# Reordering layers 0 to 2 of a four-layer graph kernel: projections, row factors, exponentials, means, tests and the next layer's features

## The chip, the cores and the metric

The kernel runs on one core of a Trainium2 chip. The metric is the device time of one execution in microseconds (us). A profile of one execution names the engines PE (TensorE, its matmuls), PEld (TensorE's loads of the stationary operand), DVE (VectorE), ACT (ScalarE), POOL (GpSimd) and SP (SyncE, which only issues transfers). L861 means line 861 of the kernel before; the program's line numbers shift a little after the change.

## The reference

The input is x, 32 batches of 512 nodes with 64 features, and one normalised adjacency matrix of 512 x 512 with few non-zero entries. Each of the four layers is `x = x + layer(relu(layernorm(x)))`:

```python
# layer 0: graph convolution
out = h @ weight_self + (adj @ h) @ weight_neighbor + bias
# layer 1: two steps of it, with a relu after each
z = relu((adj @ z) @ weights[i])            # i = 0, 1
# layer 2: graph attention
Wh = h @ W.T;  e1 = Wh @ a[:64];  e2 = Wh @ a[64:]
e   = leaky_relu(e1[:, :, None] + e2[:, None, :], 0.2)
att = softmax(where(adj > 0, e, -9e15), axis=-1)
out = elu(att @ Wh)
# layer 3 (flow): 8 heads of attention with s = (hW)(hW).T * graph, where zero
# entries are masked, then a ninth attention over the joined heads
```

All arithmetic is in float32.

## The kernel before

**Stages.** The program has two forms; the one that runs here (`fast_form`) first does layers 0, 1 and 2, some 488 us, and then layer 3, called flow, up to the end. The diff touches the first stage only, and those steps of flow that are done within it. Batches go in 16 pairs (M = 16); 512 nodes are 4 blocks (C) of 128 partitions, so that the x of a pair is 128 x 512.

**Slots.** `slot(k)` for k = 0 to 16 is one step of a pipeline written out by hand: it does layer 0 of pair k, layer 1 of pair k-2, the norm of layer 2 of pair k-3, the preparation of layer 2's attention of pair k-4 (`Gat.prepare`) and its scores and values for pair k-5 (`scores`, `values`). What PE, DVE and ACT do is in the order in which it is written (a manual schedule on these three engines); POOL only adds the bias of layer 0 (L1126). A slot may end with one more piece of work (`more`): in slots 6, 8, 10 and 12 this is `judge_rows(c)`, which tests one block of rows of the adjacency against the form that `fast_form` supposes, and in slot 15 `judge`, which brings the tests to one number.

**Drain.** After slot 16 `drain()` brings the last four pairs through layer 2; its attentions are called g2 (pair 12), g1, g0 and last (pair 15). It has fills (`fill(n)`, matmuls whose result is not used), and ahead of `last.scores(1)` it runs nine periods of flow, -10 to -2, in a loop.

**Steps and names.**
- `centre` (L857): sum of each row over its 64 features (`mean`, L861), times 1/F (L862), x minus mean (L863). It is used by the norms (`Norm.a`) and at the end of an attention (`rest`).
- `Norm.square` squares on ACT (`sq`, L881); `Spread` gathers the squares of up to four norms: `add` sums them (`var`, L899), `root` takes the square root on ACT (`std`, L906), `turn` the reciprocal (`rstd`, L914); `Norm.relu` multiplies (L885).
- `flipped` transposes on PE and copies on ACT (`ht0`, `ht2`, L310 and L312); `neighbours` multiplies by the adjacency (`nt_ps`, L921), `copied` brings this to SBUF on ACT (`nt0`, `nt1`, `nt1b`, L928); `project` multiplies by weights (L941): `po0` for layer 0, `po1a` and `po1b` for the two steps of layer 1. `po0` is added to x in the next slot (L1133), `po1b` in `ends` (L1112).
- `Gat.flip` makes `ht2`. `Gat.prepare`: features `wh_ps` (L967), 16 short matmuls on 64 rows of the array; row factors `e1` (`e_ps`, L974), two matmuls on 64 rows; then on ACT `v`, `q` and `c` (L984 to L990), of which `c` is exp of the row factors. `weigh` (L995) multiplies features by v.
- `Gat.scores` (L1005, DVE), `Gat.values` (`acc` L1018, `den` L1027, PE), `keep` (two copies on ACT, L1037), `back` (transposes to `den_ps` L1048 and `op_ps` L1053), `read` (reciprocal and product `o`, L1063 to L1066), `rest` (`e` = exp(o) on ACT, L1074; then on DVE L1077, L1078, the last of which needs e; then `centre` and a square, L1080).
- PSUM: the pool `ps_t` has four banks, which nt_ps, the transposes, wh_ps and e1 take in turn in the order in which they are written; a bank is free when the copy that reads it is done.
- Flow's `features(step)` of a batch: on ACT `less` (minus the mean, L509), x minus mean with relu (L512), times rstd (L519), times root_d (`hs`, L524); on POOL a difference `hd` (L528); on DVE a maximum `least` (L530). `make_hx` transposes hs (`hx_ps`, L310, copy L312), `make_g` multiplies (`g_ps` L550, copy L562); layer 3 begins with `s_ps` (L383), of which DVE takes maxima (L395).

Of the kernel before, what the change touches and what calls it, by code (L numbers as in the profile page):

```python
# [8 lines left out]
F32 = mybir.dt.float32  # L9
AF = mybir.ActivationFunctionType  # L10
OP = mybir.AluOpType
# [11 lines left out]
def fast_form(  # L23
# [128 lines left out]

    BC = B * C
    least = const.tile([P, BC + 1], F32, name="least")
    sound = const.tile([P, 2 + 2 * C], F32, name="sound")
    unsound = const.tile([1, 1], F32, name="unsound")
    least_out = const.tile([P, B // 2], F32, name="least_out")
    E_MAX = 5.0
# [11 lines left out]
    def scales():  # L170
# [24 lines left out]
            )  # L195
        nc.scalar.copy(urow, ps)

    def judge_rows(c):
        both, t = row_pair("edge"), row_pair("t")[:, 0]
        ok, edge = both[:, 1], both[:, 0]  # L200
        nc.vector.tensor_scalar(edge, adj_f[:, c], 0.0, None, op0=OP.not_equal)
        nc.vector.scalar_tensor_tensor(
            t, urow, root_d[:, c : c + 1], edge, op0=OP.mult, op1=OP.mult
        )
        nc.vector.tensor_tensor(t, t, adj_f[:, c], OP.subtract)
        nc.vector.scalar_tensor_tensor(t, t, -1.0, t, op0=OP.mult, op1=OP.max)
        nc.vector.scalar_tensor_tensor(
            ok, adj_f[:, c], 4e-7, t, op0=OP.mult, op1=OP.is_ge
        )
        nc.vector.scalar_tensor_tensor(  # L210
            edge, adj_t[:, c], 0.0, edge, op0=OP.not_equal, op1=OP.is_equal
        )
        nc.vector.tensor_reduce(
            sound[:, 2 + C + c : 3 + C + c], both.rearrange("p k n -> p (k n)"), AX.X, OP.min
        )


# [7 lines left out]
    def halves(k):  # L225
        return slice(k * F, (k + 1) * F)

    def row_pair(name):

        return pairs_of[0].tile([P, 2, N], F32, name=name, tag="row")  # L230
# [5 lines left out]
        return acc_of[0].tile(shape, F32, name=name, tag=acc_of[1])  # L236

    def judge():
        own = tiny.tile([P, 1], F32, name="own")
        nc.vector.tensor_reduce(own, sound, AX.X, OP.min)  # L240
        ps = acc("own_ps", [1, P])
        nc.tensor.transpose(ps, own, ident)
        nc.vector.tensor_reduce(unsound, ps, AX.X, OP.min)
        nc.vector.tensor_scalar(unsound, unsound, 0.0, None, op0=OP.is_equal)
# [244 lines left out]
    class Heads(Pair):  # L489
# [12 lines left out]
        def features(self, step):  # L502
            b = self.b
            if self.i:
                return
            mean, rstd = (t[:, b % 2] for t in flow_stats[b // 2])
            if step == 0:
                less = tiny.tile([P, C], F32, name="less")
                nc.scalar.mul(less, mean, -1.0)  # L509
                h = Heads.hn[b] = early.tile([P, C, F], F32, name="hn3", bufs=5)  # L510
                for c in range(C):
                    nc.scalar.activation(  # L512
                        h[:, c], xs[b // G][:, b % G, c], AF.Relu, bias=less[:, c : c + 1],
                        scale=1.0,
                    )
            elif step == 1:
                h = Heads.hn[b]
                for c in range(C):
                    nc.scalar.mul(h[:, c], h[:, c], rstd[:, c : c + 1])  # L519
            elif step == 2:  # L520
                h = Heads.hn[b]
                hs = Heads.hs[b] = early.tile([P, C, 2, F], F32, name="hs3", bufs=2)
                for c in range(C):
                    nc.scalar.mul(  # L524
                        hs[:, c], h[:, c, None].to_broadcast([P, 2, F]), root_d[:, c : c + 1]
                    )
# [315 lines left out]
    with (  # L842
# [14 lines left out]
        def centre(to, i):  # L857

            x4 = pair_of(i)
            mean = tiny.tile([P, 2, C], F32, name="mean", bufs=B // 2 + 12)  # L860
            nc.vector.tensor_reduce(mean, x4, AX.X, OP.add)  # L861
            nc.vector.tensor_scalar(mean, mean, 1.0 / F, None, op0=OP.mult)  # L862
            nc.vector.tensor_tensor(  # L863
                to, x4, mean[:, :, :, None].to_broadcast([P, 2, C, F]), OP.subtract
            )
            return mean

        class Norm:
# [81 lines left out]
        class Gat:  # L950
# [8 lines left out]
            def prepare(self):  # L959


                self.wh_ps = [
                    ps_t.tile([P, C, F + 1], F32, name="wh_ps", tag="ps") for k in range(2)
                ]
# [7 lines left out]
                e1 = [ps_t.tile([P, N], F32, name="e1_ps", tag="ps") for k in range(2)]  # L972
                for k in range(2):
                    nc.tensor.matmul(  # L974
                        e1[k], lhsT=wa1[halves(k), :], rhs=self.ht[halves(k), :],
                        start=True, stop=True,
                    )
                self.v = work.tile([P, 2 * C, F + 32], F32, name="v")
                self.q = tiny.tile([P, 2 * C], F32, name="q")
                self.c = row_pair("c")  # L980
                for k in range(2):
                    e2 = self.wh_ps[k][:, :, F]
                    some = slice(k * C, (k + 1) * C)
                    nc.scalar.activation(  # L984
                        self.v[:, some, F:], e2[:, :, None].to_broadcast([P, C, 32]),
                        AF.Exp, scale=0.2,
                    )
                    nc.scalar.activation(self.q[:, some], e2, AF.Exp, scale=0.8)
                for k in range(2):
                    nc.scalar.activation(self.c[:, k], e1[k], AF.Exp, scale=-0.8)  # L990
# [48 lines left out]

            def end(self):  # L1040
                self.read()
                self.rest()

            def back(self):
# [14 lines left out]
            def read(self):  # L1059
# [8 lines left out]
                    rec[:, :, :, None].to_broadcast([P, 2, C, F]), OP.mult,  # L1068
                )

            def rest(self):
                o = self.sq
                e = row_pair("e")[:, 0].rearrange("p (k c f) -> p k c f", k=2, c=C)
                nc.scalar.activation(e, o, AF.Exp)  # L1074
# [3 lines left out]
                nc.vector.scalar_tensor_tensor(x4, e, 1.0, x4, op0=OP.min, op1=OP.add)  # L1078
# [43 lines left out]
        def slot(k, more):  # L1122
# [49 lines left out]
            if n:  # L1172
                n.a()
                n.square()
                some.append(n)
            some += ended
            ended.clear()
            s = Spread()
# [10 lines left out]
            for n in some:  # L1189
                if isinstance(n, Gat):  # L1190
                    flow_stats[n.i] = n.mean, n.rstd
                else:
                    n.relu()
            if l0:
                po0[k] = project([(ht0, ws2), (nt0, wn2)], "po0")
            if u:
                u.back()
                turned.append(u)
# [13 lines left out]
        def drain():  # L1212
# [13 lines left out]
            g2.scores(1)  # L1226
            z = middle(nt1)
            g1.prepare()
            nt1b[M - 1] = neighbours(lambda c: z[:, c, :])
            s = Spread()  # L1230
            s.add(n)
# [3 lines left out]
            nt1b[M - 1] = copied(nt1b[M - 1], "nt1b")  # L1235
            g2.values()
            g2.keep()
            g1.weigh()
            s.turn()
            n.relu()  # L1240
# [7 lines left out]
            g0.flip()  # L1248
            g2.back()
            g2.read()  # L1250
            g1.scores(1)
            g0.prepare()
            fill(3)
            s = Spread()
            s.add(n)
            s.root()
            g1.values()
            g1.keep()
            s.turn()
            n.relu()  # L1260
            last = Gat(M - 1, n2.pop(M - 1).h)
# [3 lines left out]
            g0.scores(0)  # L1265
            g1.back()
            g1.read()
            last.prepare()
            g0.scores(1)
            fill(6)  # L1270
            g0.values()
# [5 lines left out]
            s.add(g2)  # L1277
            g0.back()
            g0.read()
            for i in range(-10, -1):  # L1280
                flow_period(i)
            last.scores(1)
            fill(3)
            last.values()
# [2 lines left out]
            s.add(g1)  # L1287
            last.back()
            last.read()
            last.rest()  # L1290
            fill(6)
            s.add(g0)
# [12 lines left out]
        with tc.manual_schedule(  # L1305
# [12 lines left out]
                4: scales,  # L1318
            }
            for c in range(C):  # L1320
                begun[6 + 2 * c] = lambda c=c: judge_rows(c)
            begun[7 + 2 * C] = judge
            for k in range(M + 1):
                slot(k, begun.get(k))
# [32 lines left out]
def general_form(  # L1357
# [116 lines left out]
    def stats(pool, g):  # L1474
        xg = xs[g]
        nb = G * C
        x3 = xg.rearrange("p b c f -> p (b c) f")
        mean = tiny.tile([P, nb], F32, name="mean", bufs=NG + 1)
# [437 lines left out]
```

## Time and profile before

| | us |
|---|---|
| three runs | 2078.73, 2072.11, 2077.57 |
| their median | 2077.57 |
| the profiled execution, its own time | 2077.25 |
| its span (first to last instruction) | 2075.3 |
| PE busy in the span | 1984.9 (96%) |
| DVE busy | 1748.6 (84%) |
| ACT busy | 1320.3 (64%) |
| POOL busy | 1445.5 (70%) |

The mean clock granted to PE is 0.981 of full speed. In the rows of profile below, a group or a timeline row has its start (in the timeline), busy time, engine, line, operation, output and inputs by the program's names, partitions x elements, and in brackets how long the engine was idle before it and what it waited for. "x16" means 16 instructions joined to one row. A wait row has: who waits, for what, us in total, times, the longest.

### The profile page before, as it was taken

Reading aid. Unit: us, or ns where it says so; the run is one execution under the profiler, and the core shown is the slowest. Engines: PE = TensorE matmul, PEld = TensorE weight load, DVE = VectorE, ACT = ScalarE, POOL = GpSimd, SP = SyncE. Lnnn points to the kernel's source line nnn. Section 1 sums busy time; section 2 is a strip of 40 time slices with the busy share of each in tenths; the row PEclk is TensorE's granted clock in tenths of the full one; section 3 lists DMA queues with packets and bytes.
Section 4 is the critical chain, followed back from the end, with each engine's and each line's share of the span. In section 5 each row is a group of like instructions: output and inputs, shape, how many; then the busy total and the mean of one; then the engine's idle time right before and its main releaser. Section 6 shows DMA issues by size and latency. Waiting matters only on the chain.

```text
span 2075.3 us, 29298 instructions
## 1 busy us (share of the span) xinstructions
PE 1984.9 (96%) x9374; PEld 738.2 (36%) x9374; DVE 1748.6 (84%) x4102; ACT 1320.3 (64%) x2008; POOL 1445.5 (70%) x834
## 2 busy tenths in 40 slices
PE   7999999877999999999999999999999999999995
PEld 4544445432333333333333333333333333333332
DVE  6688887667889898988888988888888988988994
ACT  3444444444676777677777777777777777776674
POOL 2000000002898989898989999998888988888996
PEclk9999999998999999999999999999999999999998
DMA  4000000001222323232223232332223222222233
GB/s 121 1 1 1 1 1 0 1 1 28 71 79 74 83 76 85 68 83 79 78 78 77 75 83 77 79 83 69 79 74 76 72 75 76 75 71 77 77 83 79
DMA packets 185876, 128.05 MB, mean 62 GB/s; under 512 B 124985, under 2 KB 130273, under 8 KB 185585
## 3 DMA queue, kind: packets, MB, share of 16 engines
q1 hardware_dynamic: 166480, 125.30, 22.4%
q10 hardware_dynamic: 18720, 0.59, 0.5%
q8 instruction: 76, 1.25, 0.3%
q14 instruction: 88, 0.71, 0.1%
q0 software_dynamic: 512, 0.20, 0.1%
HBM read 119.48 MB, written 5.37 MB: 60 GB/s over the span
## 4 chain that ended last, share of the span: by engine, by line
PE 60%; POOL 6%; DMA 4%; DVE 3%; issue 1%; ACT 1%; SPq 0%; ACTq 0%; POOLq 0%; DVEq 0%
PE s_ps L383 21%; PE av L438 20%; PE tot_ps L450 6%; PE y_ps L568 5%; POOL p_att L416 5%; PE gT_ps L613 5%; PE g_ps L550 3%; DMA topb<-top_row 2%; DVE p_att L395 2%; POOL p_att L420 1%; DVE p_att L432 1%; DMA top_row<-top 1%; PE hx_ps L310 1%; ACT e_ps L429 1%; DMA recb<-rec_row 0%
## 5 line engine op out<-in xcount | busy, mean ns | idle before, releaser
L416 POOL TENSOR_TENSOR p_att<-p_att,topb 128x1024 f32<-128x1024 f32 x429 | 1007.7, 2381 | 0.0
L395 DVE CUSTOM_DVE_ANT_0 p_att<-s_ps,flow_neg 128x512 f32<-128x512 f32 x1152 | 726.0, 685 | 96.5 <-PE s_ps L383 95.4
L383 PE MATMUL s_ps<-g,hx 64*128 64x512 f32 x2048 | 516.0, 613 | 17.1 <-DVE p_att L432 13.9
L420 POOL TENSOR_TENSOR p_att<-p_att,topb 128x512 f32<-128x512 f32 x286 | 360.5, 1281 | 170.7 <-DMA topb<-top_row 131.8
L429 ACT ACTIVATE p_att<-p_att 128x1024 f32<-128x1024 f32 x288 | 304.8, 1059 | 162.1 <-POOL p_att L420 81.4
L432 DVE TENSOR_TENSOR p_att<-e_ps,p_att 128x1024 f32<-128x1024 f32 x288 | 338.3, 1197 | 32.4 <-ACT e_ps L429 31.4
L429 ACT ACTIVATE e_ps<-p_att 128x1024 f32<-128x1024 f32 x288 | 293.0, 1029 | 79.0 <-POOL p_att L416 68.8
L383 PEld LDWEIGHTS s_ps<-g,hx 64*128 64x128 f32 x2048 | 174.9, 186 | 329.3 <-DVE top L395 175.5
L438 PE MATMUL av<-p_att,hd 128*64 128x512 f32 x1024 | 269.7, 605 | 1.1 <-DVE o_att L487 1.1
L438 PE MATMUL av<-p_att,hn 128*64 128x512 f32 x1024 | 263.3, 592 | 0.0
L1126 POOL TENSOR_TENSOR x<-x,bias_b 128x512 f32<-128x512 f32 x16 | 20.3, 1275 | 307.2 <-DVE hn L863 307.2
L586 DVE SCALAR_TENSOR_TENSOR cat<-y_ps,bh,cat 128x512 f32<-128x512 f32 x256 | 180.0, 745 | 15.5 <-ACT cat L578 14.1
L562 ACT COPY g<-g_ps 128x512 f32<-128x512 f32 x128 | 132.0, 1139 | 85.6 <-PE g_ps L550 85.6
L578 ACT ACTIVATE cat<-y_ps,bh 128x512 f32<-128x512 f32 x256 | 161.2, 681 | 36.3 <-PE y_ps L568 35.9
L450 PE MATMUL tot_ps<-p_att,ones 128*32 128x512 f32 x1152 | 155.6, 605 | 4.3 <-DVE p_att L432 4.3
L568 PE MATMUL y_ps<-o_att,wh_sb 64*128 64x512 f32 x512 | 137.5, 594 | 0.0
L613 PE MATMUL gT_ps<-cat,wo_sb 128*64 128x512 f32 x512 | 131.6, 592 | 0.0
L438 PEld LDWEIGHTS av<-p_att,hn 128*64 128x64 f32 x1024 | 73.9, 137 | 145.8 <-issue 145.8
L438 PEld LDWEIGHTS av<-p_att,hd 128*64 128x64 f32 x1024 | 62.4, 136 | 166.5 <-issue 135.9
L921 PE MATMUL nt_ps<-adj_t,hn 128*128 128x512 f32 x256 | 118.8, 608 | 0.8 <-DVE hn L885 0.8
L487 DVE TENSOR_TENSOR o_att<-av,recb 128x512 f32<-128x512 f32 x144 | 99.0, 688 | 24.4 <-DMA recb<-rec_row 23.7
L528 POOL TENSOR_TENSOR hd<-hn 128x128 f32<-128x128 f32 x32 | 14.7, 460 | 128.5 <-ACT hn L519 128.5
(192 smaller groups left out, 2190.5 us busy)
## 6 DMA issues: line engine op xcount, KB each, us to landing
topb<-top_row SPq DMA_DIRECT2D x288, 256.0 KB
recb<-rec_row SPq DMA_DIRECT2D x288, 128.0 KB
out_dram<-y SPq DMA_DIRECT2D x32, 128.0 KB
x<-in_x_dram SPq DMA_DIRECT2D x3, 1024.0 KB
top_row<-top SPq DMA_DIRECT2D x144, 4.0 KB
parts<-tot SPq DMA_DIRECT2D x144, 4.0 KB
parts<-tot ACTq DMA_DIRECT2D x144, 4.0 KB
rec_row<-rec_flow SPq DMA_DIRECT2D x144, 4.0 KB
```

The lines of the kernel that those rows point to most:

```text
L383: nc.tensor.matmul(ps[:, k], lhsT=x[halves(k), r * P : (r + 1) * P], rhs=g[halves(k), :], start=True, stop=True,)
L395: nc.vector.tensor_tensor_reduce(out=self.p[r][:, k], in0=ps[:, k], in1=flow_neg[:, r], scale=-1.0, scalar=BIG, op0=OP.add, op1=OP.min, ac ...
L416: engine.tensor_tensor(self.p[r], self.p[r], self.topb, OP.subtract)
L420: engine.tensor_tensor(p, p, self.topb[:, k], OP.subtract)
L429: nc.scalar.activation(to, self.p[r], AF.Exp, scale=-1.0)
L432: nc.vector.tensor_tensor(self.p[r], self.joined, self.p[r - 1], OP.add)
L438: nc.tensor.matmul(self.av[halves(k), :], lhsT=self.v(k, j) if j % 2 else self.less_next(k, j), rhs=self.p[j][:, k], start=(j == 0), stop= ...
L450: nc.tensor.matmul(ps[q : q + 32, :], lhsT=ones, rhs=self.p[2 * e + 1][:, k], start=True, stop=True,)
L568: nc.tensor.matmul(ps, lhsT=wh_sb[halves(k), 2 * self.i + k, :], rhs=self.o[halves(k), :], start=True, stop=True,)
L578: nc.scalar.activation(self.cat[:, k], self.y[k], AF.Identity, bias=bh01[:, h : h + 1], scale=0.01)
L586: nc.vector.scalar_tensor_tensor(self.cat[:, k], self.y[k], bh[:, h : h + 1], self.cat[:, k], op0=OP.add, op1=OP.max,)
L613: nc.tensor.matmul(self.gps[halves(k), :], lhsT=wo_sb[:, h, :], rhs=Heads.cat.pop((self.b + k, h)), start=(h == 0), stop=(h == H - 1),)
```

## The change

In a slot, the projection `po0` of layer 0 is issued ahead of `values` instead of after it. In `Gat.prepare`, the two matmuls of the row factors stand ahead of the sixteen of the features. `Gat.exp` is split off from `rest`: in a slot it comes at the same place as before, in the drain it follows `read` at once. `centre` leaves out the multiplication by 1/F, and two operations of 128 x 256 with the factor -1/F take the place of the subtraction of 128 x 512. The test of a block of rows is split into `judge_rows`, at the ends of slots 5, 7, 9 and 11, and `count_rows`, at the ends of 6, 8, 10 and 12; the counts come from accumulator outputs, so that the reduction over 1024 elements (L213) goes, and `judge` compares the counts with 512. In the drain, the nine periods of flow stand at six places instead of one.

```diff
     def judge_rows(c):
-        both, t = row_pair("edge"), row_pair("t")[:, 0]
-        ok, edge = both[:, 1], both[:, 0]
+        both = judged[c] = row_pair("edge")
+        edge, t = both[:, 0], both[:, 1]
         nc.vector.tensor_scalar(edge, adj_f[:, c], 0.0, None, op0=OP.not_equal)
         nc.vector.scalar_tensor_tensor(
             t, urow, root_d[:, c : c + 1], edge, op0=OP.mult, op1=OP.mult
         )
         nc.vector.tensor_tensor(t, t, adj_f[:, c], OP.subtract)
+
+    def count_rows(c):
+        both = judged.pop(c)
+        edge, t = both[:, 0], both[:, 1]
+        at = 2 + C + 2 * c
         nc.vector.scalar_tensor_tensor(t, t, -1.0, t, op0=OP.mult, op1=OP.max)
         nc.vector.scalar_tensor_tensor(
-            ok, adj_f[:, c], 4e-7, t, op0=OP.mult, op1=OP.is_ge
+            t, adj_f[:, c], 4e-7, t, op0=OP.mult, op1=OP.is_ge,
+            accum_out=sound[:, at : at + 1],
         )
         nc.vector.scalar_tensor_tensor(
-            edge, adj_t[:, c], 0.0, edge, op0=OP.not_equal, op1=OP.is_equal
-        )
-        nc.vector.tensor_reduce(
-            sound[:, 2 + C + c : 3 + C + c], both.rearrange("p k n -> p (k n)"), AX.X, OP.min
+            edge, adj_t[:, c], 0.0, edge, op0=OP.not_equal, op1=OP.is_equal,
+            accum_out=sound[:, at + 1 : at + 2],
         )
...
     def judge():
+        counts = sound[:, 2 + C :]
+        nc.vector.tensor_scalar(counts, counts, float(N), None, op0=OP.is_equal)
...
-                nc.scalar.mul(less, mean, -1.0)
+                nc.scalar.mul(less, mean, -1.0 / F)
...
         def centre(to, i):
             nc.vector.tensor_reduce(mean, x4, AX.X, OP.add)
-            nc.vector.tensor_scalar(mean, mean, 1.0 / F, None, op0=OP.mult)
-            nc.vector.tensor_tensor(
-                to, x4, mean[:, :, :, None].to_broadcast([P, 2, C, F]), OP.subtract
-            )
+            for k in range(2):
+                nc.vector.scalar_tensor_tensor(
+                    to[:, k], mean[:, k, :, None].to_broadcast([P, C, F]), -1.0 / F, x4[:, k],
+                    op0=OP.mult, op1=OP.add,
+                )
...
             def prepare(self):
+                e1 = [ps_t.tile([P, N], F32, name="e1_ps", tag="ps") for k in range(2)]
+                for k in range(2):
+                    nc.tensor.matmul(e1[k], lhsT=wa1[halves(k), :], rhs=self.ht[halves(k), :], ...)
                 self.wh_ps = [ ... ]
...
-                e1 = ...        # the same two matmuls, here
...
             def end(self):
                 self.read()
+                self.exp()
                 self.rest()
+            def exp(self):
+                self.e = row_pair("e")[:, 0].rearrange("p (k c f) -> p k c f", k=2, c=C)
+                nc.scalar.activation(self.e, self.sq, AF.Exp)
             def rest(self):
-                e = row_pair("e")[:, 0].rearrange("p (k c f) -> p k c f", k=2, c=C)
-                nc.scalar.activation(e, o, AF.Exp)
+                o, e = self.sq, self.e
...
         def slot(k, more):
+            if l0:
+                po0[k] = project([(ht0, ws2), (nt0, wn2)], "po0")
             some += ended
             s = Spread()
             ...                 # s.add, u.values(), s.root(), keep, weigh, s.turn, relu
-            if l0:
-                po0[k] = project([(ht0, ws2), (nt0, wn2)], "po0")
             if u:
                 u.back()
...
         def drain():
             g1.prepare()
+            flow_period(-10)
+            flow_period(-9)
...
             g2.keep()
+            flow_period(-8)
...
             g2.read()
+            g2.exp()
             g1.scores(1)
             g0.prepare()
+            flow_period(-7)
+            flow_period(-6)
             fill(3)
...
             g1.keep()
+            flow_period(-5)
...
             g1.read()
+            g1.exp()
             last.prepare()
+            flow_period(-4)
+            flow_period(-3)
             g0.scores(1)
             fill(6)
...
             g0.read()
-            for i in range(-10, -1):
-                flow_period(i)
+            g0.exp()
+            flow_period(-2)
             last.scores(1)
...
             last.read()
+            last.exp()
             last.rest()
...
+                begun[5 + 2 * c] = lambda c=c: judge_rows(c)
-                begun[6 + 2 * c] = lambda c=c: judge_rows(c)
+                begun[6 + 2 * c] = lambda c=c: count_rows(c)
```

More of the change, by code (lines that the diff above doesn't have):

```diff
@@ L154, in fast_form @@
     least = const.tile([P, BC + 1], F32, name="least")
-    sound = const.tile([P, 2 + 2 * C], F32, name="sound")
+    sound = const.tile([P, 2 + 3 * C], F32, name="sound")
     unsound = const.tile([1, 1], F32, name="unsound")
@@ L196, in scales @@
         nc.scalar.copy(urow, ps)
+    judged = {}
     def judge_rows(c):
-        both, t = row_pair("edge"), row_pair("t")[:, 0]
-        ok, edge = both[:, 1], both[:, 0]
+        both = judged[c] = row_pair("edge")
+        edge, t = both[:, 0], both[:, 1]
         nc.vector.tensor_scalar(edge, adj_f[:, c], 0.0, None, op0=OP.not_equal)
@@ L859, in centre @@
             x4 = pair_of(i)
-            mean = tiny.tile([P, 2, C], F32, name="mean", bufs=B // 2 + 12)
+            mean = tiny.tile([P, 2, C], F32, name="sum", bufs=B // 2 + 12)
             nc.vector.tensor_reduce(mean, x4, AX.X, OP.add)
-            nc.vector.tensor_scalar(mean, mean, 1.0 / F, None, op0=OP.mult)
-            nc.vector.tensor_tensor(
-                to, x4, mean[:, :, :, None].to_broadcast([P, 2, C, F]), OP.subtract
-            )
+            for k in range(2):
[3 more added lines that the diff above has]
+                )
             return mean
@@ L959, in prepare @@
             def prepare(self):
+                e1 = [ps_t.tile([P, N], F32, name="e1_ps", tag="ps") for k in range(2)]
+                for k in range(2):
+                    nc.tensor.matmul(
+                        e1[k], lhsT=wa1[halves(k), :], rhs=self.ht[halves(k), :],
+                        start=True, stop=True,
+                    )
                 self.wh_ps = [
@@ L971, in prepare @@
                         )
[L972 to L977, printed above, removed]
                 self.v = work.tile([P, 2 * C, F + 32], F32, name="v")
@@ L1069, in read @@
                 )
+            def exp(self):
+                self.e = row_pair("e")[:, 0].rearrange("p (k c f) -> p k c f", k=2, c=C)
+                nc.scalar.activation(self.e, self.sq, AF.Exp)
             def rest(self):
-                o = self.sq
-                e = row_pair("e")[:, 0].rearrange("p (k c f) -> p k c f", k=2, c=C)
-                nc.scalar.activation(e, o, AF.Exp)
+                o, e = self.sq, self.e
                 x4 = pair_of(self.i)
@@ L1477, in stats @@
         x3 = xg.rearrange("p b c f -> p (b c) f")
-        mean = tiny.tile([P, nb], F32, name="mean", bufs=NG + 1)
+        mean = tiny.tile([P, nb], F32, name="sum", bufs=NG + 1)
         nc.vector.tensor_reduce(mean, x3, AX.X, OP.add)
```

## The prediction

> **What bounds the kernel now.** The page's busy tenths and chain of waits say that from 488 us on (layer 3) PE is full and the diff touches nothing there; every edit lies in the 17 slots (they end at 398 us) or in the drain (398 to 488 us). So I read those two stretches alone: first busy time by windows, then the waits of each engine in them, then the timeline of single slots.
>
> Busy time by windows (length; busy us of PE, PEld, DVE, ACT, POOL; clock granted to PE): two slots without a test of the adjacency in the slot before, two after one, then the drain.
>
> ```profile
> 159.00:184.00 25.00, 24.78 (x130) 13.33 (x129) 20.94 (x43) 11.45 (x22) 1.28 (x1) 1.00 0.00 1
> 214.00:238.00 24.00, 23.79 (x122) 12.33 (x120) 20.27 (x42) 11.44 (x22) 1.28 (x1) 1.00 0.00 1
> 131.00:159.00 28.00, 25.57 (x120) 12.47 (x118) 24.74 (x47) 11.66 (x22) 1.27 (x1) 0.94 0.00 1
> 184.00:214.00 30.00, 27.57 (x127) 13.55 (x126) 25.26 (x48) 11.77 (x22) 1.27 (x1) 0.89 0.00 1
> 398.00:488.00 90.00, 73.66 (x343) 32.52 (x341) 54.08 (x105) 39.73 (x92) 1.36 (x3) 0.92 0.00 1
> ```
>
> PE is 99% busy in the short slots: they are PE's own length. The long ones have a lower clock and more DVE work. In the drain PE is 18% idle and DVE 40%. The waits, DVE and PE in the slots:
>
> ```profile
> DVE x L1078 <- ACT e L1074: 23.1, 11, 3.1
> DVE x L1133 <- PE po L941: 13.3, 6, 3.3
> PE e_ps L974 <- ACT nt L928: 9.0, 10, 1.9
> ```
>
> and in the drain:
>
> ```profile
> DVE x L1078 <- ACT e L1074: 24.8, 4, 11.7
> PE hx_ps L310 <- ACT hs L524: 8.3, 1, 8.3
> DVE x L1112 <- PE po1b L941: 7.0, 1, 7.0
> ```
>
> The timeline on PE shows what a long slot costs (three rows) against a short one (last two): 1.92 us of waiting, then matmuls at half clock.
>
> ```profile
> 256.64 2.07 PE L974 MATMUL e_ps<-ht,wa 64*128 64x512 f32 x2 [1.92 <-ACT nt L928]
> 258.64 5.67 PE L1018 MATMUL acc<-s,v 128*64 128x512 f32 x16
> 264.24 1.92 PE L1027 MATMUL den<-s,v 128*32 128x512 f32 x16
> ...
> 363.25 1.12 PE L974 MATMUL e_ps<-ht,wa 64*128 64x512 f32 x2 [0.21 <-ACT nt L928]
> 364.31 3.65 PE L1018 MATMUL acc<-s,v 128*64 128x512 f32 x16
> ```
>
> From den_ps (L1048) of slot 5 (105.77) to that of slot 15 (371.63) are 265.86 us: 24.54 in a short slot, about 28.7 in a long one, mean 26.59. The cause of a long slot is in DVE: a test (L201 to L213) took 237.90 to 243.06 in one piece, which makes L1133 and all behind it late.
>
> [...] 5.67 against 3.65 us above, and the drops start at 150.0, 201.2, 255.8 and 310.4 us[...]. [...] where the four e_ps matmuls come together (410.32 us) they take 1.08 us, against 1.07 plus 1.12 above. [...] The trace shows 0.76 us of idle PEld at such a change, but no gap in PE (73.20 + 1.08, next at 74.21). [...] The trace has 1.28 alone: load at 352.74, exp at 354.03.
>
> **The change part by part.**
>
> *po0 ahead of acc, e1 ahead of wh (slots).* PE's work stays; its order after po1a becomes e1, wh, po0, acc, den, den_ps. e1 now takes PSUM banks that are free early, so its two matmuls run together (1.08). wh takes the banks that wait for ACT's copies of ht0 and nt0; queued behind it on PE are po0, acc, den. In a short slot, from den_ps = 0: po1a starts at 12.95, and nt0's copy ends at 16.11 (hn 14.22 to 14.91, behind it sq 15.01, then the copy). With two means less in front (0.24) it ends at 15.87. Then wh 15.95 to 17.05, po0 to 19.15 (its 2.1 us), acc 3.6 to 22.73, den, and den_ps 2.63 after den's start, as in slot 16, which has no po0 (395.00 to 397.62, 0.71 of it waiting for kept). Sum **25.35**, that is 0.8 longer than a short slot, 3.3 shorter than a long one. PE idles 0.95 ahead of wh and 0.7 ahead of den_ps.
>
> *L1133.* It no longer waits for po0 (13.3 us, 6 times), for po0 ends some 6 us before den_ps. DVE then waits at L1078 instead: that wait ends with e, which is timed by PE (nt1b 4.3 us after den_ps, copy, sq, table load 1.28, exp 0.63: 7.60). So this gains only where DVE was late.
>
> *Tests split.* Before: 418 + 751 + 692 + 692 + 684 + 1220 ns in one slot of two. After: 1.86 us in one slot, 2.07 in the next; two accumulator reads of about 0.08 (78 ns at L174) are added and the 1.22 reduce goes. DVE has 20.3 to 20.9 busy in a short slot (which holds no test); 22.8 at most fits in 25.35. Cover: the wait at L1078, up to 3.15 us. If it is gone, 2 us in each of 8 slots, 16 us: the same as what the long slots lose now. The judge's extra operation on 128x8 (0.17 by the L862 row) stands ahead of its 7.4 us wait for own_ps at the end of slot 15, once: nothing, or 0.2.
>
> *Shorter means.* L862 (174 ns, 64 times) goes; L863 (0.69, next start 0.61 later) becomes two 128x256 operations, by the L1112 row 0.75. About 0.14 each: 9 us of DVE, on the path only as counted above and in the drain.
>
> *Slots summed.* All ten at 25.35 would give 253.5, −12. [...] I let it fall in a quarter to half of the slots at 1.6 us[...]: 26.0 on average, 260, **−6**. Bounds: −12; and, if both mode changes cost 0.76 on PE, 26.9 or +3, with a drop in every slot +19. Slot 5, whose acc did not wait before, loses 0.7 (po0 +2.1 ahead of acc, −1.1 behind it, 0.2 of waiting, −0.5 for shorter means); slot 16, without po0, gains 0.4 from its means.
>
> *exp ahead of copies (drain).* e follows o at once on ACT instead of standing behind kept and copies. *Flow's features spread (drain).* Each batch issues on ACT 0.19 + 1.06, 1.05 and 1.26 us (L509 to L524), on POOL one hd (0.45, idle otherwise), on DVE one least (0.41), on PE the hx transposes (2.2 for two batches, at half clock) and g_ps; no transfer is issued, so no queue of SP changes. Two batches are done before layer 3 and f0 of two more. Today they stand in one block, and behind them stood
>
> ```profile
> 463.98 2.21 PE L310 MATMUL hx_ps<-ident,hs 128*128 128x128 f32 x8 [8.29 <-ACT hs L524]
> ...
> 472.65 3.65 PE L1018 MATMUL acc<-s,v 128*64 128x512 f32 x16
> ...
> 479.38 0.69 DVE L1078 SCALAR_TENSOR_TENSOR x<-e,x 128x512 f32<-128x512 f32 x1 [11.72 <-ACT e L1074]
> ```
>
> Laid out by hand with these durations: f0 and f1 push the root std from 434.2 to 436.5; behind it are rstd, relu 437.5 and flip. L1078 of the second Gat comes at 438.85 instead of 441.56. hx waits for ACT's copies of c of the last Gat, which stand behind exp, at 446.75; queued behind hx are fill(6) and acc, so acc comes at 453.05 instead of about 448, and rec stays near 460.6. From there it gains: last.scores(1) ends about 465.5 (before 467.0), and acc follows it at 466 instead of 472.65, as hx, g_ps and features are done. I take the last maxima 8 to 10 us before today's 488.32: **−9** (bounds −3, if std and hx are later still, and −12, if hx doesn't wait).
>
> Sum: −6 + 0.7 − 0.4 − 9 = −14.7, say −14. The profiled execution took 2077.25 us (span 2075.3), the median is 2077.57: **2063 us**. Layer 3 then only starts earlier.
>
> **The rivals.** *Slots gain nothing*: clock drops in every second slot[...] give 26.6 a slot; drain −9: 2068. *Slots at PE's length*: no drop, 25.35, drain −12: −24, 2053. *Drain given back*: features delay std, and hx (idle 3.9 us ahead of it, clock halved) delays acc; drain −3, slots as forecast: 2069; with slots at nothing 2075, no measurable change. *Slower*: po0 in front of acc. The new path nt0 copy, wh, po0, acc, den, den_ps has no slack, and the 0.95 idle ahead of wh halves the clock in each slot (+1.7) while both mode changes cost PE 0.76: 28.5 a slot, +19; with the drain's −9, 2088. It decides from 27.5 a slot (26.59 plus 9/10); slower by 0.3% from 28.1. For it: after 1.92 idle the clock did fall in four long slots. Against it: 0.21 idle never did it, and no PE gap at mode changes is seen. *It does not do what it says*: L1133 still waits, if po0 is late. Excluded only by po0's new place, 6 us earlier.
>
> **How the numbers follow.** Some 0.3%, 6.2 us, is what a measurement of this kernel can tell from no change. Forecast (2056 to 2071) 0.42; slots at PE's length 0.14; slots gain nothing 0.15; drain given back 0.16, of it half above 2071; slower path 0.13, of it 0.10 beyond 2083.8. Faster by over 0.3% (below 2071.3): 0.42 + 0.14 + half of 0.15 and 0.16, some 0.71; slower 0.10; within 0.19. The range, 2048 to 2078, leaves out the slower path and little below.
>
> **What would show it.** Right: L1133 waits for nothing; L1078's wait in slots up to 3 to 5 us; den_ps every 25 to 26 us, with no 28.7; e_ps as x4 in 1.08; acc 3.6; the last maxima at about 473 to 476; hx's wait under 4 us, the 11.72 gone. Wrong: wh with waits over 1.5 us and acc at 5.6 in most slots (the slower path); L1112 or relu waiting for PE or std in the drain; den_ps distances over 27.

## The result, and the profile after

The changed kernel takes 2056.89 us (median of four runs, 2053.16 to 2057.64); the kernel before, on the same chip, 2078.15. The ratio is 0.9896, 95% interval 0.9867 to 0.9924, so 21 us less. Line numbers differ a little: in after, L1090 is the old L1078, L1145 the old L1133, L973 the row factors (old L974), L982 the features (old L967), L1058 the old L1048, L1083 the exponential e (old L1074), L937 the copy of nt (old L928).

Busy time by windows, kernel after (columns as before: length, PE, PEld, DVE, ACT, POOL, clock): two neighbouring slots, each with a half of a test, and the stretch from slot 16's den_ps to layer 3's second maximum (the second of DVE's maxima of s_ps), which is called the drain below.

```profile
156.84:181.95 25.11, 23.80 (x124) 13.05 (x124) 21.81 (x45) 11.68 (x22) 1.28 (x1) 1.00 0.00 1
181.95:207.06 25.11, 23.80 (x124) 13.05 (x124) 21.94 (x47) 11.68 (x22) 1.28 (x1) 1.00 0.00 1
381.92:466.32 84.40, 72.90 (x344) 33.42 (x344) 54.33 (x106) 40.23 (x93) 1.37 (x3) 0.94 0.00 1
```

All slots are alike now, and the clock is full in each (1.00 from 106.61 to 357.76 us, against 0.96 over the ten slots of before). The waits of the ten slots (106 to 358 us), DVE's and then PE's:

```profile
DVE x L1090 <- ACT e L1083: 32.1, 10, 4.6
...
PE den_ps L1058 <- ACT kept L1046: 7.8, 11, 0.7
PE wh_ps L982 <- ACT nt L937: 6.1, 10, 0.6
```

The addition at the slot's start (L1145) waits no more; DVE waits for e instead, longer than before. PE has two short waits in each slot, which the timeline shows in place:

```profile
321.51 1.13 PE L973 MATMUL e_ps<-ht,wa 64*128 64x512 f32 x4
322.47 0.33 PE L982 MATMUL wh_ps<-wgv,ht 64*128 64x65 f32 x2
323.41 1.10 PE L982 MATMUL wh_ps<-wgv,ht 64*128 64x65 f32 x14 [0.61 <-ACT nt L937]
326.43 3.65 PE L1027 MATMUL acc<-s,v 128*64 128x512 f32 x16
330.01 1.92 PE L1036 MATMUL den<-s,v 128*32 128x512 f32 x16
332.64 0.66 PE L1058 MATMUL den_ps<-ident,kept 128*128 128x128 f32 x4 [0.71 <-ACT kept L1046]
```

The four row factor matmuls run together (1.13), wh waits 0.61 for nt0's copy, den_ps 0.71 for kept, and acc has its 3.65. In the drain, from the timeline of PE and a wait of DVE:

```profile
432.07 1.97 PE L318 MATMUL hx_ps<-ident,hs 128*128 128x128 f32 x8 [3.91 <-ACT c L999]
433.83 6.78 PE L1222 MATMUL fill_ps<-adj_t,ident 128*128 128x512 f32 x12
440.54 3.65 PE L1027 MATMUL acc<-s,v 128*64 128x512 f32 x16
```

```profile
DVE rec L1073 <- PE den_ps L1058: 12.1, 3, 7.3
```

hx's wait has fallen from 8.29 to 3.91 and now stands ahead of the values of g0. The clock is at half from 430.0 to 436.8 us, which slows hx (1.97, against 1.09 in a run below) and the first 3 us of the fill (6.78, against 5.42 for the same fill before). The wait of 11.72 for e is gone; DVE waits 7.3 for den_ps of g0 in its place.

Where the 20.6 us between the two spans come from, by marks in both timelines:

| stretch | before | after | difference |
|---|---|---|---|
| start to den_ps of slot 5 | 105.77 | 106.61 | +0.84 |
| ten slots, den_ps of slot 5 to 15 | 265.86 | 251.15 | −14.71 |
| slot 16 | 25.99 | 24.16 | −1.83 |
| drain, den_ps of slot 16 to second maximum | 90.70 | 84.40 | −6.30 |
| layer 3, from there to the end | 1587.0 | 1588.4 | +1.4 |

### The profile page after: what moved, and what is told of

The parts are those of the page before. It is cut to its first block, busy times and chain, and to the rows that moved or that the text cites. A ratio compares the mean times of both kernels' runs of the same rounds, so it can differ in the third digit from the quotient of the medians.

```text
span 2054.7 us, 29214 instructions
## 1 busy us (share of the span) xinstructions
PE 1966.7 (96%) x9374; PEld 738.0 (36%) x9374; DVE 1736.7 (85%) x4107; ACT 1321.5 (64%) x2008; POOL 1446.0 (70%) x834
## 4 chain that ended last, share of the span: by engine, by line
PE 75%; DVE 8%; POOL 6%; ACT 5%; DMA 4%; issue 2%; SPq 0%; ACTq 0%; POOLq 0%; DVEq 0%
PE s_ps L391 22%; PE av L446 20%; PE tot_ps L458 6%; PE y_ps L576 5%; POOL p_att L424 5%; PE gT_ps L621 5%; PE nt_ps L930 4%; PE g_ps L558 3%; PE acc L1027 3%; DVE s L1014 2%; DMA topb<-top_row 2%; PE den L1036 1%; DVE p_att L403 1%; PE po L950 1%; DVE p_att L440 1%
## 5 line engine op out<-in xcount | busy, mean ns | idle before, releaser
L1138 POOL TENSOR_TENSOR x<-x,bias_b 128x512 f32<-128x512 f32 x16 | 20.4, 1277 | 292.3 <-DVE hn L871 292.3
L464 ACT COPY tot<-tot_ps 128x512 f32<-128x512 f32 x144 | 83.2, 578 | 32.3 <-PE tot_ps L458 31.5
```

## Experiments

The measured quantities are those of the table: ten slots, and drain. They come from one profile of each kernel. The ten slots repeat well (251.1 to 251.2 in three profiles with the slots of the kernel after); the drain varies, by amounts given below. A total is the median, and a ratio is to the kernel before on the same chip.

### What made the long slots

The change has four edits in the slot: po0's place, prepare's order, the split of the tests, the means. Each run below is of the kernel after with one or two of them undone, or of the kernel before with one alone. **Theory A** says that a whole test makes DVE late, which starts a chain up to PE; **B**, that po0's move was the cure; **C**, prepare's order.

First, po0 back at its old place in the kernel after:

```diff
-            if l0:                       # ahead of values
-                po0[k] = project(...)
...
+            if l0:                       # behind relu, ahead of back
+                po0[k] = project(...)
```

> The kernel after, with po0 back behind the norms' relu (ahead of den_ps), all else as changed. Measured quantity: distance from den_ps of slot 5 to den_ps of slot 15, 251.15 us in the profile after (25.11 a slot), 265.86 before (26.59). Theory A, the long slots of before came from DVE being late through a whole test in one slot, and splitting it cured that: PE has 23.8 us of work a slot, 0.6 of waiting ahead of wh stays, and the 0.7 ahead of den_ps is filled by po0, so about 24.4 a slot, 244 in ten, and the total some 7 us under the kernel after. Theory B, moving po0 cured it, for the addition at the slot's start waited up to 3.3 us for po0 and made DVE late: with po0 late that wait is back, 2 us of test behind it, and the slots that follow a test are 27 to 29 us again, 258 to 266 in ten, the total 7 to 15 us above the kernel after.

Measured: 24.19 a slot, 241.86 in ten, 2047.19 us, ratio to before 0.9844 (0.9827 to 0.9861). As A said, and shorter than it said (24.4): without po0's move the changed kernel is 10 us *faster*, and no slot is long. The waits (DVE's, then PE's, ten slots) show that the addition hardly waits for po0 even so:

```profile
DVE x L1145 <- PE po L950: 0.7, 2, 0.3
...
PE wh_ps L982 <- ACT nt L937: 6.1, 10, 0.6
```

Second, prepare's order undone (wh ahead of e1).

> The kernel after, with features ahead of row factors in prepare as before, all else as changed. Theory A (lateness of DVE, whatever its cause, made the long slots): the second row factor matmul waits for nt0's copy, which ends 15.87 us after den_ps, when PE comes to it at about 15.95, so no wait and a slot of 25.1 to 25.2, ten slots 251 to 252, total unchanged. Theory C (the order inside prepare removed the idle that halved the clock): e_ps waits 1 to 2 us for the copy again and the clock falls in some slots, ten slots 258 or more, total 7 us or more above the kernel after. In the drain the order may cost or save up to 1 us, as wh instead of e1 then waits for the transposes.

Measured: 25.13 a slot, 251.31 in ten, 2058.1 us. As A; C falls: the order of the matmuls in prepare moves the wait from one instruction to another and is worth 0.02 us a slot here. In the drain it does more. This run's drain took 82.08, less than in any of the five profiles that have the new drain unchanged (83.5 to 84.4, below). The timeline of PE at its start shows why, in the kernel after (first row) and with wh ahead of e1 (second row):

```profile
398.24 5.40 PE L930 MATMUL nt_ps<-adj_t,z 128*128 128x512 f32 x8 [2.68 <-ACT c L999]
396.96 3.70 PE L930 MATMUL nt_ps<-adj_t,z 128*128 128x512 f32 x8 [2.62 <-ACT c L999]
```

The wait is nearly the same, but with e1 ahead of wh the clock falls behind it (at 399.2 us), and nt_ps takes 5.40 instead of 3.70. So the new order of prepare, which gains nothing in the slots here, makes this group of the drain 1.7 us longer. The total of this run is not lower for it; its slot 16 took 25.64 us instead of 24.16, and the other stretches vary too.

Third, both halves of a test in one slot, po0 early:

```diff
-                begun[5 + 2 * c] = lambda c=c: judge_rows(c)
-                begun[6 + 2 * c] = lambda c=c: count_rows(c)
+                begun[6 + 2 * c] = lambda c=c: (judge_rows(c), count_rows(c))
```

> The kernel after, with both halves of a test in one slot (slots 6, 8, 10, 12), 3.9 us of DVE in one piece; the reduction stays away. Theory A (the split cured the long slots): the slots after a test are 27 us or longer, their clock falls, ten slots 258 or more, total 7 us or more above the kernel after. Theory B (po0's move did; DVE has 4.6 us of waiting for e in a slot without a test): 3.9 us fit into that wait, every slot stays at 25.1, ten slots 251 to 252, total unchanged.

Measured: 25.11 and 25.19 in turn, 251.41 in ten, 2056.89 us. This is as B said and not as A did: with po0 early a whole test of 3.9 us, without its reduction, does fit. So far either of two edits, the split or po0's move, seemed able to cure the long slots; the next two runs try each alone on the kernel before.

> The kernel before, with po0 alone moved ahead of values; means, tests, prepare and drain as before. Theory B (po0's move is what cures the long slots): the addition at the start of a slot waits no more, the whole test of 4.5 us nearly fits into the wait for e (4.6 in the kernel after, some 4.3 with the longer means), so slots of 25.4 to 25.7, at most 1 us more after a test, ten slots 254 to 260, no half clock, total 2077 less 6 to 12. Theory A or C (tests or prepare's order cured it): the slots after a test stay at 28 to 30 us and the others grow from 24.5 to 25.3, ten slots 266 to 272, total 0 to 6 us above the kernel before.

Measured with po0's move alone: 25.47 in slots without a test, 27.0 or 28.6 after one, 264.06 in ten, 2084.4 us, ratio 1.0018 (1.0012 to 1.0025). That lies between the two forecasts for the slots: the move takes 1.8 off the ten slots and makes every slot without a test 0.92 longer. The profile is that of the fastest of twenty executions (2077.59), so it can't show what makes the median longer. The timeline of PE of a slot after a test still has the wait and a slowed acc (the clock fell in two of the four such slots, those of 28.6 us: 0.94 on average from 181.79 to 210.38 and from 235.85 to 264.47 us):

```profile
253.62 1.12 PE L974 MATMUL e_ps<-ht,wa 64*128 64x512 f32 x2 [1.77 <-ACT nt L928]
257.74 4.17 PE L1018 MATMUL acc<-s,v 128*64 128x512 f32 x16
```

> The kernel before with the split of the tests alone (halves of 1.9 and 2.1 us in slots 5 to 12, the reduction over 1024 elements gone); po0, prepare, means and drain as before. Theory A, a whole test makes DVE late, and that alone makes slots long and the clock fall: every slot takes 24.5 us like those without a test before, the ten from den_ps of slot 5 to that of slot 15 take 245.4 instead of 265.9, the clock stays full, and the total is some 20 us under the kernel before, about the whole gain of the change. Rival D, it takes the shorter means as well (three in a slot, 0.4 us): slots with half a test take 25 to 26.5 and some halve the clock, ten slots 250 to 258, total 8 to 15 us under the kernel before.

Measured with the split alone: 24.54 in every slot, 245.43 in ten, acc 3.65 in each, as at full clock, 2058.91 us, ratio 0.9898 (0.9874 to 0.9922). A slot of this run by the windows:

```profile
177.31:201.85 24.54, 24.32 (x126) 12.86 (x125) 22.35 (x47) 11.45 (x22) 1.28 (x1) 1.00 0.00 1
```

The edit of the tests alone gains about what the whole change gains, with the drain still the old one; rival D falls. That edit does two things, it splits a test and it drops the reduction of 1.22 us. A whole test, without the reduction, put back with po0 late:

> The kernel after with po0 late (24.19 us a slot when run before) and, on top, both halves of a test in one slot (3.9 us of DVE). Theory A: the norm that starts the next slot ends 2 us later than with a half, its square on ACT stands ahead of e and makes e some 1.1 us late, wh waits 1.7 instead of 0.6: four slots of 25.2 or more, and 27 to 28 where the clock then halves; ten slots 246 to 256 instead of 241.9, total 4 to 14 us above po0 late alone (2047). Rival E, the reduction of 1.22 us and the longer means made the lateness, not the test in one piece: ten slots stay at 242 to 243, total unchanged against po0 late.

Measured: 25.19 after the first test, 26.88 after the other three, 250.98 in ten, 2055.61 us. As A; E falls as it was stated (242 to 243): a test in one piece costs 9.1 us in the ten slots. But these slots are still far from the 265.86 of the kernel before, so the reduction and the longer means have a part in its long slots. How the 20.4 us that the edit of the tests gains on the kernel before divide between the split and the dropped reduction is not shown, as neither was run there alone. The timeline shows the chain, on ACT and then, in the same slot, on PE:

```profile
183.27 0.63 ACT L890 ACTIVATE sq<-hn 128x512 f32<-128x512 f32 x1 [0.91 <-DVE hn L871]
183.92 1.28 ACT L1083 ACT_TABLE_LOAD   x1
185.21 0.63 ACT L1083 ACTIVATE e<-o 128x512 f32<-128x512 f32 x1
```

```profile
194.11 1.10 PE L982 MATMUL wh_ps<-wgv,ht 64*128 64x65 f32 x14 [1.62 <-ACT nt L937]
195.14 5.35 PE L1027 MATMUL acc<-s,v 128*64 128x512 f32 x16
```

The test delays the norm at the next slot's start (hn); its square on ACT waits 0.91 for it; the table load and e stand behind that square, so e, the second addition, the next norm, nt0's copy and wh are each 1.0 late (wh waits 1.62 instead of 0.61); and after 1.61 to 1.62 us of idle acc takes 5.35 instead of 3.65 in three slots of the four, as it did in before with the clock at half from 150.1 to 153.5 us. The kernel before has the same chain: the square waits at 245.48, e runs at 247.42, e_ps waits 1.92.

Last, the means, with po0 late:

```diff
-            for k in range(2):
-                nc.vector.scalar_tensor_tensor(to[:, k], ..., -1.0 / F, x4[:, k], ...)
+            nc.vector.tensor_scalar(mean, mean, 1.0 / F, None, op0=OP.mult)
+            nc.vector.tensor_tensor(to, x4, mean..., OP.subtract)
```

> The kernel after with po0 late (24.19 us a slot) and the means as before (a multiplication on 128x8 and one subtraction of 128x512). Two means stand in the chain from e to nt0's copy, 0.14 us each: wh waits 0.88 instead of 0.60, 24.4 to 24.5 a slot, ten slots 244 to 245, total 2 to 4 us above po0 late. Rival: half a test then makes DVE late as well (rival D), slots after a second half take 25 us or more, ten slots 248 or more, total 7 us or more above.

Measured: 24.53 a slot, 245.27 in ten, 2050.66 us; wh waits 0.95, and acc takes 3.65 in each of the ten slots, as at full clock. That is 0.34 a slot, just above the 0.2 to 0.3 expected; the rival falls.

These runs give the ten slots step by step, each a measured pair: 265.86, edit of the tests −20.43 (245.43), prepare's order −0.16 (245.27; this kernel also has the new drain, which lies behind the ten slots), means −3.41 (241.86), po0 early +9.29 (251.15). What a step is worth depends on its place in this order: po0's move on the kernel before took 1.8 off.

### The drain

The nine periods of flow in one block, exp still early:

> The kernel after with the nine periods of flow in one block ahead of last.scores(1), as before; exp still follows read at once. Measured quantity: second maxima of layer 3 after den_ps of slot 16, 84.4 us in the kernel after, 90.7 before. Laid out with the durations of after: values of g0 come some 7 us earlier (433.5 instead of 440.5), as hx no longer stands ahead of them, then features of two batches take 7.4 us of ACT after e of g0, hx and g_ps follow, and values of last come at 455 to 457 instead of 451.6: drain 88 to 90, total 4 to 5 us above the kernel after. Theory F, spreading the features is the drain's whole gain: drain 90 to 91. Theory G, exp's place is: drain 84 to 85, total unchanged.

Measured: drain 89.09, 2062.23 us. As laid out: values of g0 come at 431.42, 52.5 after slot 16's den_ps (58.6 in the kernel after), and hx then waits for hs again:

```profile
446.07 2.21 PE L318 MATMUL hx_ps<-ident,hs 128*128 128x128 f32 x8 [7.34 <-ACT hs L532]
```

Spreading the features is worth 4.7 us, with exp early. Exp late again, features spread:

> The kernel after with exp inside rest in the drain, as before; the features of flow stay spread. Theory G, exp's place is the drain's gain: second maxima 88 to 91 us after den_ps of slot 16 (84.4 in the kernel after), total 4 to 6 us above. By hand: e of g2 comes 3 us later and g0's first scores with it, but c of last no longer stands behind e of g1 on ACT, so hx comes 2 to 3 us earlier and values of g0 too; the two offset each other and the drain takes 82 to 86, total within 2 us of the kernel after.

Measured: drain 87.05, 2064.78 us. Neither forecast was met: exp's place is worth 2.65 us, with the features spread. hx did not come earlier (50.1 us after slot 16's den_ps in both kernels), and on ACT e of g1 stood behind the copies of g0's values (DVE waits 8.4) and e of g0 behind those of last (4.0). The waits of DVE (390 to 470 us):

```profile
DVE x L1090 <- ACT e L1083: 17.2, 3, 8.4
```

In this run layer 3 took 1593.4 us, against 1587.0 to 1591.3 in the others; why is open (its first s_ps are interleaved with the values of last).

### What lies beyond

If PE's two waits are all that is left in a slot, moving nt1b should take both away:

```diff
+            if l1:
+                nt1b[k - 2] = neighbours(lambda c: z[:, c, :])
             if u:
                 u.back()
                 turned.append(u)
-            if l1:
-                nt1b[k - 2] = neighbours(lambda c: z[:, c, :])
```

> The kernel after (po0 early) with one more move in a slot: the matmuls of nt1b stand ahead of the transposes den_ps and op_ps instead of behind them. Theory H, two waits of PE are all that is left in a slot of the kernel after (0.71 ahead of den_ps for kept, 0.61 ahead of wh for nt0's copy): the 3.4 us of nt1b cover the first, and e on ACT, which stands behind nt1b's copy, comes some 1.6 us earlier, which takes the second away: 23.8 us a slot, PE's own work, against 25.11, ten slots 238 to 239, total some 13 us under the kernel after, 2042 to 2046. Rival I, o becomes late, as op_ps now comes 3.4 us after den instead of 0.7, and e follows it: wh still waits 0.6 or more, 24.4 a slot or longer, ten slots 244 or more, total at most 7 us under the kernel after.

Measured: 23.51 a slot, 235.15 in ten, 2035.29 us, ratio 0.9801 (0.9777 to 0.9825). Theory H, and more than it forecast (23.8, and 2042 to 2046 in all): the ten slots give 16.0 us. What the rest of the program adds was not followed up; den_ps itself comes later in a slot here, so the first stretch and the drain can't be compared with the others. PE is busy throughout (windows, this kernel):

```profile
177.66:201.17 23.51, 23.51 (x125) 12.93 (x124) 21.99 (x46) 11.70 (x22) 1.28 (x1) 1.00 0.00 1
```

Then hx behind the values of g0, with po0 late:

```diff
-            flow_period(-4); flow_period(-3)     # behind last.prepare()
...
             g0.keep()
+            flow_period(-4); flow_period(-3)
```

> The kernel after with po0 late (2047 us, drain 83.5 from den_ps of slot 16 to the second maxima) and the periods -4 and -3 of flow, which hold the transposes hx, behind keep of g0 instead of behind prepare of last. Theory: hx's wait of 3.9 us for c of last, its 2 us at half clock and the slow fill hold up values of g0; with hx behind them these come 6 us earlier (as in the run with flow in one block, where they came 52.5 us after den_ps of slot 16 instead of 58.6), the wait of rec for den_ps (7.3) shrinks to 1 or 2, and all that follows comes 5 to 6 us earlier: drain 77 to 79, total 2041 to 2043. Rival: hx then holds up den_ps of g0 or g_ps of flow's first heads, values of last wait for it, and the drain keeps 82 to 84, total unchanged at 2047.

Measured: drain 77.40 instead of 83.54, as the theory said; the total, 2037.39 us, fell by more than the drain's 6.1, and the rest is open. In the timeline of PE hx waits for nothing, and the fill and the values take 5.42 and 3.65, as at full clock.

```profile
418.16 5.42 PE L1222 MATMUL fill_ps<-adj_t,ident 128*128 128x512 f32 x12
423.51 3.65 PE L1027 MATMUL acc<-s,v 128*64 128x512 f32 x16
427.09 1.92 PE L1036 MATMUL den<-s,v 128*32 128x512 f32 x16
428.95 1.09 PE L318 MATMUL hx_ps<-ident,hs 128*128 128x128 f32 x8
```

> The kernel after with both moves: nt1b ahead of den_ps in the slots (23.51 us a slot when run alone, second maxima 77.8 us after den_ps of slot 16) and hx behind keep of g0 in the drain (worth 6.1 us there, 83.5 to 77.4). Theory: the two lie in different stages and add up: 23.5 a slot, second maxima 71 to 73 us after den_ps of slot 16, total 2035 less 6, 2028 to 2031. Rival: g0's values come so early that the drain is then bound by DVE's chain of scores, means and reads, and only 2 to 3 us of the 6 arrive: 75 to 76, total 2032 to 2034.

Measured with both moves: 23.51 a slot, second maximum 71.3 us after den_ps of slot 16, **2030.4 us** (2028.14 to 2034.98), ratio to before 0.977 (0.9751 to 0.9789). As the theory said, they add up, and this version is 26 us under the kernel after.

## Why the prediction was right, and where not

The direction and the size hold (2063 forecast, range 2048 to 2078, 2056.89 measured), but its two main terms were off in opposite directions, the larger one in its favour, so that the sum came this near is in part luck.

- **L1133's wait goes, DVE waits for e instead: right, but it gains nothing.** 13.3 us are gone, and e's wait is up to 4.6 (forecast 3 to 5). In the trace of before the six waits of L1133 stand at 106, 159, 214, 268, 323 and 347 us, all at starts of slots with no test ahead of them. Where DVE was late it never waited for po0.
- **A slot of 25.35: right, 25.11.** The copy of nt0 ends 15.83 after den_ps (forecast 15.87). The wait ahead of wh is 0.61 instead of 0.95, as the first two of wh's matmuls run ahead of it (0.33). den_ps's 0.71 came as taken from slot 16. The mode changes (from 128-row to 64-row matmuls and back) leave no gap on PE that shows: po1a runs from 320.53 for 1.05 us and e_ps starts at 321.51, wh runs from 323.41 for 1.10 and po0 starts at 324.44.
- **Slots summed, −6: mis-sized, −14.7.** The term that failed is "I let it fall in a quarter to half of the slots": the clock fell in none of the ten slots of the profile after. That it might at 0.95 of idle, and its price, were the author's estimates. It fell in nine of the twelve slots in which PE waited 1.6 to 1.9 ahead of wh or e_ps (before four of four, po0 alone two of four, whole test with po0 late three of four, there by acc's 5.35), and in none with 0.6 to 1.0 there (after 0.61, old means 0.95; acc 3.65). A fall took 1.69 in the run of the whole test with po0 late (26.88 against 25.19). A reading was off too: a long slot of before is not about 28.7 but 28.71, 29.89, 29.98 and 30.03 us, 29.65 on average, so the four lost 20.5 against short ones and not 16.
- **What made the gain: not split up far enough.** The prediction summed po0, prepare and tests as one slot of 25.35. Its own working had po0's order 0.8 us longer than a short slot; the runs make that a loss of 9.3 us in ten slots, while the edit of the tests, for which it asked only whether the two halves fit in, gives 20.4. It had named the whole test as the cause of the long slots, but gave taking that cause away no price of its own. po0's move could gain only where DVE was late, and DVE is not late once tests are split.
- **Shorter means: size right.** 0.14 each, in the chain twice: 0.34 a slot was measured, the forecast of the run with old means 0.2 to 0.3.
- **Slot 5, +0.7, and slot 16, −0.4.** The first mark moved by +0.84, but stands at 102.95 to 105.94 in the kernels with po0 late, and at 103.5 to 106.6 in those with po0 early and nt1b in its place, so nothing follows. Slot 16 took 24.1 to 27.1 us in eight profiles of kernels with the new means and nt1b in its place, so the −1.83 may be chance. In the profile after, po1a waits 3.94 in this slot and the clock stands at half behind it, from 371.9 to 375.3 us; what decides the slot's length was not tried.
- **Drain, −9: right in mechanism, −6.3 in these two profiles.** hx waits 3.91 (forecast 3.9) and std delays rstd (2.6), both as laid out; L1112's wait for po1b, named as a sign of being wrong, was 6.6, but it was 7.0 before. From hx's start to acc it took 8.47 us and not 6.30, as hx and a part of the fill ran at half clock. The slower nt_ps that came with prepare's order (1.7) was not in the layout. rec of g0 came 65.5 after den_ps of slot 16 instead of the 63.0 forecast. The old drain varies by itself: it took 93.11 and 93.03 in the runs with po0 or the split alone, against 90.70 in the profile of before; the new one took 83.5 to 84.4 in the five profiles that have it unchanged and nt1b in its place. Against the mean of the old three (92.3) the gain is 7.9 to 8.8.
- **The slower path.** Its price was real (0.92 a slot) and its place right, but the half clock it needed did not come: 25.11 stayed far below the 27.5 from which it would have decided.
- **Layer 3 only starts earlier: right within 1.4 us**, and that is within what it differs by in these runs (1587.0 to 1591.3, and 1593.4 once).

## What to carry to other kernels

Ask of a piece of work that is "in the slack" whether it fits into the slack in one piece and where in the queue it stands: five microseconds of DVE at a slot's start went through a square on ACT, a table load and an exp before PE stood still, and the cure was to shorten them and cut them in two, not to move PE's work. Price each edit of a bundle alone against the best slot that the trace of before already has (24.54 here), not against the mean: an edit that makes the good slots longer then shows as a loss even if the bundle gains. Look at each place where the same code stands: the order inside prepare that was worth nothing in a slot made a group of the drain 1.7 us longer. Short waits of PE that came in every slot were taken away here by independent matmuls put in front of the waiter: with nt1b's 3.4 us ahead of den_ps both of them were gone, and a slot was 1.6 us shorter.

## What the runs showed of the hardware

In the ten slots of before the clock stood at half (0.50) in four stretches: 3.41 us from 150.10, and 6.83 us each from 201.30, 255.91 and 310.53. In each of these slots PE waited 1.92 or 1.93 for nt, and the fall at 201.30 us came only 1.01 us into a wait that began at 200.29. In the run of the whole test with po0 late acc took 5.35 instead of 3.65 behind a wait of 1.61 to 1.62 us ahead of wh, in three of four slots. Behind the waits of 0.61 (after) and 0.95 (old means) ahead of wh acc took 3.65 in each of the twenty slots.

The length of the wait alone does not decide. One wait of 1.61 us, in the first of those four slots, was followed by an acc of 3.65. At the start of the drain PE waits 2.6 to 2.9 us for c in each profile. With wh ahead of e_ps the nt_ps behind this wait took 3.70 in all four profiles (before, po0 alone, split alone, wh first); with e_ps ahead of wh it took 5.13 to 5.40 in eight, and 3.70 in the two in which nt1b had been moved. The cause of the difference is open: these runs do not show what makes the clock fall.

The read of an accumulator output took 0.08 us (79 to 82 ns, L214 and L218 of after). The operations themselves took as long with the output as without (medians of 692 and 684 ns with it, 692 and 684 without, L207 and L210 of before).
